# A three-layer block on one core: the recurrence's terms laid out apart, plain gathers with sums on VectorE, late weights issued by SyncE, and new durations for the order of instructions

## The chip, the cores and the metric

The kernel runs on one core of one Trainium2 chip. The metric is the device time of one execution in microseconds (us); lower is better. Everything is float32 except a few small masks. Five engines of the core each run their own list of instructions in order: PE (TensorE, matrix products and transposes), DVE (VectorE), ACT (ScalarE), POOL (GpSimd) and SP (SyncE, which here issues DMAs and reads registers). Each engine waits at an instruction until its inputs are there, and everything behind that instruction in its list waits too.

## The reference

An input x of 8 sequences by 512 positions by 128 channels passes through four residual layers: a gated-delta recurrence, a mixture of experts, a linear attention and the same mixture of experts again. Each layer sees a layer norm of x.

```python
# layer a: 16 heads of 8 channels; q, k, v pass a 4-tap causal convolution and silu; q and k are normalised
def step(S, inp):                                   # S: 8 x 8 per sequence and head
    q_t, k_t, v_t, b_t = inp
    v_new = (v_t - einsum('bhd,bhdm->bhm', k_t, S)) * b_t[..., None]
    S = S + einsum('bhd,bhm->bhdm', k_t, v_new)
    return S, einsum('bhd,bhdm->bhm', q_t, S)
...
# layers f and g: the two best of 8 experts for each row
topw, topi = top_k(softmax(xt @ Wg), 2)
topw = topw / sum(topw)
h = relu(einsum('nd,edf->enf', xt, W1)); y = einsum('enf,efd->end', h, W2)
out = einsum('ne,end->nd', combine, y)              # combine holds topw at topi
...
# layer b: linear attention of 16 heads with phi = elu + 1, causal
num = (tril(phi_q phi_k^T)) v + phi_q S;  den = the same with ones for v;  out = num / den
...
x = x + a(norm(x)); x = x + f(norm(x)); x = x + b(norm(x)); x = x + f(norm(x))
```

## The kernel before

**Tiling.** The 512 positions are cut into eight chunks of 64. A chunk of all eight sequences is 512 rows, held as a tile `x_a` of 128 partitions by 4 by 128. In the recurrence the 128 partitions are the 8 x 16 pairs of sequence and head instead, and the data of a chunk pass through DRAM (`scr`, `scb`, `sco`) to change between the two layouts.

**Streams.** The work is written as Python generators: `preparing` (norm, convolutions, the recurrence's factors, one chunk after another), `recurring` (the recurrence itself), and four `layers` lanes, each of which takes two chunks through the layers f, b and g. A generator yields the name of the engine that it needs next. `Weaver.run` (L97) takes, again and again, the stream that could start first by a clock that it keeps for each engine, using the durations of the function `duration` (L180) and ranks for ties. So the order of instructions on every engine is fixed when the program is built; on the chip each engine follows it. `Slots` hands out named buffers, and a stream that finds none free waits until one is given back.

**Preparing** (L491 to L682). `prepare(c)` loads `x_a`, takes the norm (`bn_stats` on DVE, four small `rs` operations on POOL, `xn` on ACT), transposes it, and multiplies it by four shifted weights `wc` for each of q, k and v (`s_pp_a`, tags s = 0, 1, 2), with `beta` beside it. Each result `y_a` goes out to `scr` and comes back as `qk` or `vv`. ACT then writes the squares `sq` and the turned copies `kq`. DVE forms the norms `nrm`, the factors `W`, and couples the four tokens of each step through the tiles `spare` and `kk`; two products of the second coupling run on POOL (L628). Products of queries and keys (`of_q`, L640) use the same tile tag `t8`. After chunk 0 `load_later_weights` (L326) issues, all on ACT's queue, the expert weights `w` to DRAM, the attention weights `wb`, `wob`, `bob`, and twelve blocks of zeros to the expert row buffers `there`. The six issues of `w` come from L329 and L331, the small weights from L334 to L336, the zeros from L355.

**Recurring** (L702 to L790). Four tokens make a step and four steps a group, so a chunk has four groups and the kernel 128 steps. The state is kept per group in one tile `st[p, step, term, m, d]` with five terms: four updates and the old state. Each step is four DVE instructions in a chain: product `pj`, its sum into `factors` (PSUM), the updates `st[:, s, 0:4]`, and a sum over the five terms into the next step's state:

```python
terms = st[:, s].rearrange("p i m d -> p m d i")
dve.tensor_reduce(st[:, s + 1, TK], terms, AX.X, ALU.add)
```

A term has 8 x 8 numbers, so the five numbers of one sum lie 256 bytes apart. `outputs` (L756) then copies the last state into its own group and the factors into `vn`, both on ACT; POOL multiplies states by queries into `po`, and DVE sums `po` into `o`. `ending` (L792) adds the corrections (`oc`), normalises (`so`, `rms`, `on`) and sends the result through `sco` to `oT`.

**Experts** (`moe`, L928). Each chunk's rows are sorted by expert: eight indirect DMAs on POOL scatter weighted rows `xw` to `there`; SP loads them back as `xs` in blocks; PE multiplies each block by its expert's weights `wt`, which SP fetches by register; the results go to `back`, and eight indirect DMAs gather them and add them to `x_a` in flight (L1189). Of the sixteen layers f and g, thirteen run so; g6, f7 and g7 run all experts densely (`all_experts`, L833) with weights that stay in SBUF. Each sorted layer owns one of three sets of buffers `m`.

**Attention** (`attend`, L1209). Per 128 rows POOL forms the products `kv`, PE multiplies them by a triangular matrix, DVE by the queries. `keep` (L1312) adds the chunk's keys and values to the running state `sbd`: DVE masks into `up`, POOL adds.

All four instructions of a step, all products and nearly every other instruction are issued through `Timed` and carry its line, L166; the profile's groups are told apart by tile names.

Of the kernel before, what the change touches and what calls it, by code (L numbers as in the profile page):

```python
# [179 lines left out]
def duration(key, op, args, kw):  # L180
# [6 lines left out]
    if key == "PE":  # L187
        if op == "transpose":
            return key, 0.16, 0.15
        return key, max(free_size(args[2]) * 1.95e-3, 0.32), 0.15  # L190
# [4 lines left out]
    if key == "ACT":  # L195
        table = TABLE_OF.get(args[2]) if op == "activation" else None
        return key, (0.39 if "bias" in kw else 0.2) + n * 0.76e-3, 0.1, table
    if key == "POOL":
        return key, 0.15 + n * (1.8e-3 if n > 512 else 2.2e-3), 0.1
    if op == "reciprocal":  # L200
        return key, 0.06 + n * 7.6e-3, 0.0
# [4 lines left out]
def kernel(  # L206
# [119 lines left out]
    def load_later_weights():  # L326
        for half in range(2):
            es = slice(half * NE // 2, (half + 1) * NE // 2)
            nc.scalar.dma_start(w12[es, :, 0:NF], f_w1[es])  # L329
            for f in range(2):  # L330
                nc.scalar.dma_start(  # L331
                    w12[es, :, NF + f * D : NF + (f + 1) * D], f_w2[es, f * P : (f + 1) * P, :]
                )
        nc.scalar.dma_start(wb, b_wT)  # L334
        nc.scalar.dma_start(wob, b_woT)
        nc.scalar.dma_start(bob, b_bo.to_broadcast([P, D]))  # L336
        nc.gpsimd.memset(earlier, 1.0)
# [12 lines left out]
        zero = slots.tile([P, 4 * D], F32, tag="m00", name="zero")  # L350
        nc.gpsimd.memset(zero, 0.0)
        for xd, _ in rows_by_expert:
            for g in range(0, NBK, 4):
                n = min(4, NBK - g)
                nc.scalar.dma_start(  # L355
                    blocks(xd)[:, g : g + n, :],
                    zero[:, 0 : n * D].rearrange("p (i d) -> p i d", i=n),
                )


    def held_in(n, shape, key, pool_=slots):
        return Slots(weaver, pool_, shape, key, n)

    banks = held_in(GENERAL, [P, 512], "s", ps)
    long_banks = held_in(7 - GENERAL, [P, 512], "y", ps)
    ys = held_in(2, [P, NB, CH], "y")
    sts = held_in(2, [P, SUB + 1, TK + 1, HD, HD], "st")
    pjs = held_in(2, [P, SUB, TK, HD, V1], "pj")
    pos = held_in(2, [P, 2, SUB, HD, HD], "po")
    mns = held_in(2, [P, 2 * D], "mn")  # L370
    phs = held_in(3, [P, 2 * D], "ph")
    vs = Slots(weaver, None, None, "v", 3, v1s)
    kvs = held_in(2, [P, NH, HD, HD], "kv")
    qss = held_in(1, [P, (NH + 2) * HD * HD], "qs")
    qTs = held_in(2, [P, P], "qT")
    nds = held_in(2, [P, ND + NH], "nd")
    dns = held_in(2, [P, NH], "dn")
    ups = held_in(2, [P, ND + NH], "up")
    xsTs = held_in(3, [P, HB * P], "xsT")
    hTs = held_in(3, [P, HB * P], "hT")  # L380
    ybs = held_in(2, [P, HB, D], "yb")
    xns = held_in(LANES + 1, [P, HB, D], "xn")
    ms = [held_in(3, [P, HB, D], f"m{i}") for i in range(SETS)]
    wts = held_in(SETS * WTS, [P, 2 * NF], "wt")
    ahead = [Slots(weaver, None, None, "ahead", AHEAD, list(range(AHEAD))) for _ in range(SETS)]
    sets = Slots(weaver, None, None, "set", SETS, list(range(SETS)))
# [104 lines left out]
    def prepare(c):  # L491
# [27 lines left out]
        sq = pair.tile([P, 2, CH, HD], F32, tag="t8", name=f"sq_{c}", bufs=1)  # L519
# [19 lines left out]
        def convolved(s):  # L539
            pp = yield from banks.take(f"pp_{n}_{s}")  # L540
# [16 lines left out]
            if s < 2:  # L557
                yield "ACT"
                act.activation(sq[:, s].rearrange("p t d -> p d t"), qk[:, s], AF.Square)
# [5 lines left out]
        landed = [spawn(beta())] + [spawn(convolved(s)) for s in (1, 0, 2)]  # L565
        qn, kn = kq[:, 0], kq[:, 1]
        for e in landed[1:3]:
            yield e
        yield "DVE"
        dve.tensor_reduce(nrm, sq, AX.X, ALU.add)  # L570
        yield "DVE"
        dve.tensor_scalar(nrm, nrm, ATT_A_EPS * ATT_A_EPS, None, ALU.max)
# [8 lines left out]
        nbr = pair.tile([P, CH], F32, tag="nbr", name=f"nbr_{c}", bufs=1)  # L581
        yield landed[0]
        yield "DVE"
        dve.scalar_tensor_tensor(br, be, 1.0, rk, ALU.add, ALU.mult)
        dve.scalar_tensor_tensor(nbr, br, -2.0, rk, ALU.mult, ALU.mult)
        yield "DVE"
        W = pair.tile([P, CH, 2 * HD], F32, tag="W", name=f"W_{c}")
        dve.tensor_tensor(W[:, :, 0:HD], kn, nbr.unsqueeze(2).to_broadcast([P, CH, HD]), ALU.mult)
        yield landed[3]
# [9 lines left out]
        spare = pair.tile([P, 2 * CH, HD], F32, tag="t8", name=f"spare_{c}", bufs=1)  # L599
        w01 = spare[:, 0:CH].rearrange("p t d -> p (t d)").rearrange("p (s d) -> p s d", s=NP)  # L600
        pr = spare[:, CH : CH + NP]
# [12 lines left out]
        pr = spare[:, 0:CH].rearrange("p (s i j) d -> p s i j d", i=2, j=2)  # L614
        for i in range(2):
# [8 lines left out]
        taken = [  # L624
            spare[:, i * CH : (i + 1) * CH].rearrange("p (s i w) d -> p s i (w d)", i=2, w=2)
            for i in range(2)
        ]
        for j in range(2):  # L628
            yield "POOL"
            pool.tensor_tensor(  # L630
                taken[j], W4[:, :, j, :].unsqueeze(2).to_broadcast([P, NS, 2, 2 * HD]),
                kk2[:, :, :, j].unsqueeze(3).to_broadcast([P, NS, 2, 2 * HD]), ALU.mult,
            )
        for j in range(2):
            yield "DVE"
            dve.tensor_tensor(W4[:, :, 2:4, :], W4[:, :, 2:4, :], taken[j], ALU.add)
# [3 lines left out]
        def of_q():  # L640
            pq = spare[:, 0:CH].rearrange("p (i s) d -> p i s d", i=TK)
# [10 lines left out]

    def preparing():
        yield spawn(weights_of_taps())
        for c in range(NCH):
# [6 lines left out]
            if c == 0:  # L662
                load_later_weights()
                spawn(centred(wg[:, 0:NE], NE, "wg"))
                spawn(centred(wb, 3 * D, "wb"))
# [7 lines left out]
        t = pair.tile([P, 2 * CH, HD], F32, tag="t8", name="w8", bufs=1)  # L673
        flat += [t[:, i * CH : (i + 1) * CH].rearrange("p t d -> p (t d)") for i in range(2)]
# [27 lines left out]
    def recurring():  # L702
        after = yield from sts.take("0_0")
        nc.vector.memset(after[:, 0, TK], 0.0)
        for c in range(NCH):
# [5 lines left out]
            vn = pair.tile([P, NS, TK, HD], F32, tag="vn", name=f"vn_{c}", bufs=1)  # L711
# [4 lines left out]
            for g in range(NS // SUB):  # L716

                s0 = g * SUB
                st = after
                last = c + 1 == NCH and g + 1 == NS // SUB  # L720
                if not last:
                    after = yield from sts.take(f"{c}_{g + 1}")
# [33 lines left out]
                def outputs(  # L756
                    st=st, c=c, g=g, s0=s0, op=op, qnp=qnp, vn=vn, vg=vg,
                    copied=None if last else after
                ):
                    if copied is not None:  # L760
                        yield "ACT"
                        act.copy(st[:, SUB, TK], copied[:, 0, TK])
                    yield "ACT"
                    act.copy(vn[:, s0 : s0 + SUB], vg)
# [19 lines left out]
                    yield from all_of([spawn(output(i)) for i in range(2)])  # L784
                    sts.give(st)
# [4 lines left out]
            spawn(ending(c, vn, o, op, nrm, qk, summed), -99)  # L790

    def ending(c, vn, o, op, nrm, qk, summed):  # L792
# [644 lines left out]
```

## Time and profile before

| | us |
|---|---|
| median of 3 runs (1055.51 to 1066.51) | 1059.97 |
| the profiled execution | 1058.37 |
| its span, first to last instruction | 1056.6 |

Mean granted TensorE clock in it: 0.82 of full speed. Busy time of the engines in stretches of the span, from the windows view (us):

| stretch | PE | DVE | ACT | POOL |
|---|---|---|---|---|
| 0 to 76 | 21.2 | 28.5 | 17.8 | 15.4 |
| 76 to 160 | 31.9 | 72.2 | 38.0 | 30.8 |
| 160 to 260 | 70.4 | 85.8 | 45.6 | 50.6 |
| 260 to 360 | 57.1 | 74.9 | 52.3 | 63.0 |
| 360 to 460 | 69.5 | 78.5 | 42.4 | 61.4 |
| 460 to 560 | 74.1 | 81.3 | 50.7 | 74.6 |
| 560 to 660 | 78.1 | 70.3 | 47.1 | 55.3 |
| 660 to 760 | 66.5 | 66.3 | 48.6 | 72.9 |
| 760 to 860 | 65.9 | 63.0 | 43.0 | 54.6 |
| 860 to 960 | 78.5 | 26.2 | 34.5 | 63.4 |
| 960 to 1057 | 76.9 | 24.5 | 31.6 | 23.1 |

How to read the lines: in a group of instructions, `out<-in` are the tiles by name, then the shapes and the count; after the first bar stand the busy time and the mean length of one in ns; after the second the idle time of the engine just before them, with what ended most of it. `SPq` and `ACTq` are DMA issues by those engines. A digit in the slices is the busy share in tenths of one of 40 equal slices of 26.4 us. The chain of waits is followed back from the last instruction, at each step to what released it, so its shares say what the end of the program hung on.

### The profile page before, as it was taken

Reading aid. Unit: us, or ns where it says so; the run is one execution under the profiler, and the core shown is the slowest. Engines: PE = TensorE matmul, PEld = TensorE weight load, DVE = VectorE, ACT = ScalarE, POOL = GpSimd, SP = SyncE. Lnnn points to the kernel's source line nnn. Section 1 sums busy time; section 2 is a strip of 40 time slices with the busy share of each in tenths; the row PEclk is TensorE's granted clock in tenths of the full one; section 3 lists DMA queues with packets and bytes.
Section 4 is the critical chain, followed back from the end, with each engine's and each line's share of the span. In section 5 each row is a group of like instructions: output and inputs, shape, how many; then the busy total and the mean of one; then the engine's idle time right before and its main releaser. Section 6 shows DMA issues by size and latency. Waiting matters only on the chain.

```text
span 1056.6 us, 12737 instructions
## 1 busy us (share of the span) xinstructions
PE 690.0 (65%) x3282; PEld 460.7 (44%) x3282; DVE 671.4 (64%) x1719; ACT 451.6 (43%) x1112; POOL 565.2 (53%) x626
## 2 busy tenths in 40 slices
PE   5114246667448597487678677748676807999867
PEld 2001116335446266277236565536345807444333
DVE  2538989789878489787879675648896411531610
ACT  3214264463526436366355454453533523434222
POOL 1212443654484835855892648785875275844230
PEclk9657577877768787798889988789688957999969
DMA  1252054343454542766443655764335555211010
GB/s 33 87 177 72 21 159 140 80 128 115 142 130 157 114 130 72 205 197 164 111 116 103 203 162 132 207 166 149 88 110 176 165 155 142 58 30 60 10 61 10
DMA packets 161097, 125.18 MB, mean 118 GB/s; under 512 B 45984, under 2 KB 126976, under 8 KB 161024
## 3 DMA queue, kind: packets, MB, share of 16 engines
q1 hardware_dynamic: 132640, 105.27, 33.8%
q0 software_dynamic: 18304, 13.64, 7.0%
q10 hardware_dynamic: 10080, 5.45, 1.7%
q8 instruction: 26, 0.43, 0.2%
q14 instruction: 47, 0.39, 0.1%
HBM read 90.98 MB, written 35.44 MB: 120 GB/s over the span
## 4 chain that ended last, share of the span: by engine, by line
DVE 32%; PE 22%; POOL 21%; issue 9%; ACT 6%; DMA 5%; ACTq 2%; another core or an unknown queue 1%; SPq 1%; POOLq 0%; DVEq 0%
POOL x_a L166 9%; DVE st L166 6%; PE y_py_g L166 4%; PE s_ph_g L166 4%; POOL po L166 4%; PE s_pp_a L166 3%; POOL there L166 3%; DVE factors L166 3%; PE s_pc_b L166 2%; DVE pj L166 2%; DVE nd_b L166 2%; DVE W L166 2%; DVE qs_b L166 2%; PE y_py_f L166 2%; DMA m_xs_g<-there 2%
## 5 line engine op out<-in xcount | busy, mean ns | idle before, releaser
L166 POOL TENSOR_TENSOR po<-st,kq 128x256 f32<-128x256 f32 x128 | 95.2, 871 | 68.0 <-DVE st L166 36.7
L166 PE MATMUL s_pc_b<-kv_b,tri 128*128 128x512 f32 x128 | 78.8, 730 | 38.9 <-POOL kv_b L166 38.6
L166 POOL DMA_INDIRECT x_a<-back,rows_f x56 | 88.3, 1576 | 17.9 <-issue 16.8
L166 PE MATMUL s_pp_a<-xnT_a,wc 128*128 128x512 f32 x192 | 97.6, 646 | 0.0
L166 DVE TENSOR_REDUCE st<-st 128x64 f32<-128x320 f32 x128 | 89.8, 701 | 3.8
L166 DVE TENSOR_REDUCE o<-po 128x64 f32<-128x512 f32 x64 | 43.5, 681 | 67.0 <-POOL po L166 67.0
L166 POOL DMA_INDIRECT x_a<-back,rows_g x48 | 75.1, 1564 | 17.6 <-issue 14.2
L166 PE MATMUL y_py_f<-wt_f,hT_f 128*128 128x128 f32 x420 | 65.3, 310 | 23.5 <-ACT hT_f L166 21.8
L166 POOL TENSOR_TENSOR kv_b<-ph_b,v 128x1024 f32<-128x1024 f32 x32 | 65.0, 2096 | 28.2 <-DVE ph_b L166 23.3
L166 POOL DMA_INDIRECT there<-m_xw_f,rows_f x56 | 56.2, 1004 | 31.8 <-issue 12.5
L166 PEld LDWEIGHTS y_py_f<-wt_f,hT_f 128*128 128x128 f32 x420 | 58.5, 218 | 27.8 <-ACT hT_f L166 24.4
L166 ACT ACTIVATE hT_g<-s_ph_g 128x512 f32<-128x512 f32 x80 | 46.3, 583 | 50.8 <-PE s_ph_g L166 49.0
L166 POOL TENSOR_TENSOR sbd<-sbd,up_b 128x144 f32<-128x144 f32 x48 | 27.5, 617 | 72.8 <-DVE up_b L166 72.6
L166 POOL DMA_INDIRECT there<-m_xw_g,rows_g x48 | 48.1, 1003 | 32.2 <-ACT m_xw_g L166 21.1
L166 DVE TENSOR_REDUCE factors<-pj 128x32 f32<-128x288 f32 x128 | 58.8, 459 | 9.7 <-ACT vn L166 5.6
L166 PE MATMUL s_ph_f<-xsT_f,wt_f 128*128 128x128 f32 x420 | 62.4, 303 | 1.8 <-ACT xsT_f L166 1.0
L166 DVE TENSOR_TENSOR qs_b<-s_pc_b,ph_b 128x512 f32<-128x512 f32 x64 | 43.1, 684 | 31.4 <-PE s_pc_b L166 31.4
L166 PE MATMUL s_pt_g<-ident,m_xs_g 128*128 128x128 f32 x106 | 21.8, 346 | 61.0 <-DMA m_xs_g<-there 59.5
L166 PE MATMUL y_py_g<-wt_g,hT_g 128*128 128x128 f32 x360 | 52.1, 297 | 14.2 <-ACT hT_g L166 14.1
L166 PEld LDWEIGHTS s_ph_f<-xsT_f,wt_f 128*128 128x128 f32 x420 | 57.4, 214 | 7.0 <-issue 2.9
L166 ACT ACTIVATE hT_f<-s_ph_f 128x512 f32<-128x512 f32 x72 | 40.5, 576 | 43.6 <-PE s_ph_f L166 35.5
L166 DVE TENSOR_TENSOR st<-factors,kq 128x256 f32<-128x256 f32 x128 | 54.0, 422 | 4.6 <-issue 1.3
(299 smaller groups left out, 1722.0 us busy)
## 6 DMA issues: line engine op xcount, KB each, us to landing
wt_f<-w SPq DMA_DIRECT2D x105, 256.0 KB
wt_g<-w SPq DMA_DIRECT2D x90, 256.0 KB
scr<-y_a SPq DMA_DIRECT2D x24, 256.0 KB
m_xs_f<-there SPq DMA_DIRECT2D x21, 256.0 KB
back<-yb_f SPq DMA_DIRECT2D x21, 256.0 KB
m_xs_g<-there SPq DMA_DIRECT2D x18, 256.0 KB
back<-yb_g SPq DMA_DIRECT2D x18, 256.0 KB
qk<-scr SPq DMA_DIRECT2D x16, 256.0 KB
```

What stands on the lines that cost most here:

```text
L166: r = call(*args, **kw)
```

## The change

1. `duration`: a transpose 0.2 us instead of 0.16, POOL's power 1.05, a reciprocal 0.15 + 6.5 ns per element, `bn_stats` 0.28.
2. The late weights become a stream on SP; small weights first, then `w`, then the zeros. The memsets that stood among them become part of this stream. The centring of `wb` waits for its load.
3. The state tile is `st[p, term, step x m x d + 16]`, read through `by_step`. The five numbers of one sum now lie 336 numbers, 1344 bytes, apart.
4. The convolutions run in the order keys, values, beta, queries, and wait for the taps' weights, which are formed beside the first norm. Norms of keys and queries are formed apart. The tag `t8` is split in two, `t80` and `t81`; four buffers `y` instead of two.
5. The coupling products `spare` run on DVE.
6. In the recurrence the copy of the last state goes from ACT to POOL, and `vn` is copied 2 us later by the weaver's clock. `vn` is taken once the chunk before has used its own; `oc` takes the tag `so`; `oT` has two buffers instead of three. `ending` waits for the chunk before to reach `delta`, and `sco` for `added` two chunks before.
7. The gathers go to buffers `g` without accumulation, and DVE adds each of the two to `x_a`.
8. The attention's running state is added on DVE, for both halves at once.

```diff
-    sts = held_in(2, [P, SUB + 1, TK + 1, HD, HD], "st")
+    sts = held_in(2, [P, TK + 1, (SUB + 1) * HD * HD + 16], "st")
+    def by_step(t):
+        t = t[:, :, 0 : (SUB + 1) * HD * HD]
+        return t.rearrange("p i (s m d) -> p s i m d", s=SUB + 1, m=HD)
...
+    def loading_later_weights():
+        for w, by in ((wb, b_wT), (wob, b_woT), (bob, b_bo.to_broadcast([P, D]))):
+            yield "SP"
+            sp.dma_start(w, by)
+        fire("wb")
...
+                yield "SP"
+                sp.dma_start(w12[es, :, to], by)
+                weaver.took("SP", 1.5)
...
+                yield "SP"
+                sp.dma_start(blocks(xd)[:, g : g + n, :], zero[:, 0:n, :])
...
-        landed = [spawn(beta())] + [spawn(convolved(s)) for s in (1, 0, 2)]
+        landed = [spawn(convolved(1)), spawn(convolved(2)), spawn(beta()), spawn(convolved(0))]
...
-            yield "POOL"
-            pool.tensor_tensor(
-                taken[j], W4[:, :, j, :].unsqueeze(2).to_broadcast([P, NS, 2, 2 * HD]),
+            yield "DVE"
+            dve.tensor_tensor(
+                taken, W4[:, :, j, :].unsqueeze(2).to_broadcast([P, NS, 2, 2 * HD]),
...
-                        yield "ACT"
-                        act.copy(st[:, SUB, TK], copied[:, 0, TK])
+                        yield "POOL"
+                        pool.tensor_copy(st[:, SUB, TK], copied[:, 0, TK])
...
+        if c > 0:
+            yield fired("delta", c - 1)
...
         for k in range(2):
+            g = yield from m_.take(f"g_{name}_{k}")
             for at in range(HB):
                 yield "POOL"
                 pool.indirect_dma_start(
-                    out=xt[:, at, :], out_offset=None, in_=yd,
+                    out=g[:, at, :], out_offset=None, in_=yd,
...
-                    compute_op=ALU.add,
...
+            def add(g=g, back=back):
+                weaver.goes_on(back)
+                yield "DVE"
+                dve.tensor_tensor(xt, xt, g, ALU.add)
+                m_.give(g)
...
-                        yield "POOL"
-                        pool.tensor_tensor(sb, sb, up, ALU.add)
-                        ups.give(up)
+                if c > 0:
+                    yield "DVE"
+                    dve.tensor_tensor(sb, sb, up, ALU.add)
+                    ups.give(up)
```

## The prediction

> **What bounds the kernel now.** The page's busy table and its forty slices come first, then the chain that ended last.
>
> ```profile
> PE 690.0 (65%) x3282; PEld 460.7 (44%) x3282; DVE 671.4 (64%) x1719; ACT 451.6 (43%) x1112; POOL 565.2 (53%) x626
> ...
> PE   5114246667448597487678677748676807999867
> DVE  2538989789878489787879675648896411531610
> ...
> POOL 1212443654484835855892648785875275844230
> ...
> DVE 32%; PE 22%; POOL 21%; issue 9%; ACT 6%; DMA 5%; ACTq 2%; another core or an unknown queue 1%; SPq 1%; POOLq 0%; DVEq 0%
> ```
>
> No engine is full over the whole span, and the slices show three stages. Up to slice 3 (76 us) little runs. From 76 to 560 us DVE is the fullest: the windows view gives it 72.2 of 84, 85.8, 74.9, 78.5 and 81.3 of each 100 us. From 560 to 860 us nothing is full (DVE 70, 66, 63; PE 78, 67, 66 per 100) and engines wait for each other in their fixed orders. After 860 us PE has 155 of 197 us. The chain passes between DVE, PE and POOL accordingly.
>
> Which groups the chain is made of:
>
> ```profile
> POOL x_a L166 9%; DVE st L166 6%; PE y_py_g L166 4%; PE s_ph_g L166 4%; POOL po L166 4%; PE s_pp_a L166 3%; POOL there L166 3%; DVE factors L166 3%; PE s_pc_b L166 2%; DVE pj L166 2%; DVE nd_b L166 2%; DVE W L166 2%; DVE qs_b L166 2%; PE y_py_f L166 2%; DMA m_xs_g<-there 2%
> ...
> L166 POOL DMA_INDIRECT x_a<-back,rows_f x56 | 88.3, 1576 | 17.9 <-issue 16.8
> ...
> L166 DVE TENSOR_REDUCE st<-st 128x64 f32<-128x320 f32 x128 | 89.8, 701 | 3.8
> L166 DVE TENSOR_REDUCE o<-po 128x64 f32<-128x512 f32 x64 | 43.5, 681 | 67.0 <-POOL po L166 67.0
> ...
> L166 POOL DMA_INDIRECT there<-m_xw_f,rows_f x56 | 56.2, 1004 | 31.8 <-issue 12.5
> ...
> L166 POOL TENSOR_TENSOR sbd<-sbd,up_b 128x144 f32<-128x144 f32 x48 | 27.5, 617 | 72.8 <-DVE up_b L166 72.6
> ```
>
> The accumulating gathers into x are the largest entry (9.1% in the chain view, 96 us); each holds POOL 1576 ns, a plain scatter 1004. A reduce of 320 elements takes 701 ns, more than one of 512 (681). POOL stands 72.6 us for `up` before `sbd`, with `po` products behind it, and DVE stands 67.0 us for `po`.
>
> Last, the timeline of the start:
>
> ```profile
> 46.32 0.65 ACTq L329 DMA_DIRECT2D w<-in_f_w_dram  x1
> ...
> 47.01 4.36 ACTq L331 DMA_DIRECT2D w<-in_f_w_dram  x2
> ...
> 51.40 3.19 ACTq L329 DMA_DIRECT2D w<-in_f_w_dram  x1
> ...
> 54.64 4.71 ACTq L331 DMA_DIRECT2D w<-in_f_w_dram  x2
> ...
> 59.39 2.93 ACTq L334 DMA_DIRECT2D wb<-in_b_wT_dram  x1
> ...
> 63.37 7.69 ACTq L355 DMA_DIRECT2D there<-zero  x12
> ...
> 73.31 0.69 DVE L166 TENSOR_REDUCE o<-po 128x64 f32<-128x512 f32 x1 [15.34 <-POOL po L166]
> ```
>
> ACT issues DMAs from 46.3 to 71.1 us. The copy of `st`, which POOL needs for `po`, is queued behind them, so DVE stands 15.3 us in the first recurrence. The four rs operations of chunk 1 are queued on POOL behind that `po` and start at 73.36, though their input is there at 57.4.
>
> **What the Trainium skill says.** (1) "SBUF — State Buffer", Door 1: SBUF has 16-byte lines, and an access that always goes to a new line pays. Within the trace this fits the 256-byte reads of the reduce, and also strided writes: `W<-vv` (64-byte steps) 1079 ns and `on` (256-byte) 1046, against 690 for a contiguous 512. By that sentence 1344 bytes is no better than 256. (2) "GPSIMD Engine Reference", 4.1 Engine selection: two-input elementwise work is about twice as slow on GpSimd as on VectorE. The trace says 1.6 times (`spare<-W,kk` 1142 on POOL, 697 on DVE). (3) The SBUF page, Who interferes with whom: a VectorE instruction with two SBUF inputs and a GpSimd one that reads SBUF block each other. `po` takes 714 ns at least and 871 in the mean, which agrees. (4) "DMA: Bandwidth & Descriptors", Issuing engines are not separate DMA queues: moving an issue to another engine saves sequencer time only. Here that time is ACT's 24 us.
>
> **The change part by part.** Sums are against the profiled execution, 1058.4 us (its span is 1056.6), 1.6 below the median of the runs, 1060.0.
>
> Start. The six `w`, three small weights and twelve zero blocks go from ACT to SP. The 15.3 us stall goes. Chunk 0's first steps also shorten: the third tap product (1.1) is no longer ahead of the statistics, beta's matmul (1.9) no longer ahead of the keys, keys and values no longer wait for the queries (`W` some 2 earlier), and `spare` stays on DVE (0.7): about 5.5. In the other direction, SP's order places a `w` (2.3, from 4.71/2) before chunk 1's keys and one of 3.2 before its values: +5. The zero blocks come after chunk 1's queries in SP's order, some 90 us in, and the first scatter at 143.9 needs them, so they are hidden; the memsets (2.5 us on POOL) lie beside the second recurrence group. Net -16, bounds -5 to -28 (chunk 1's transposes, at 75.9 now, could come as early as 60).
>
> Reduce of `st`. No read at 1344 bytes is in the trace. From 459 ns (288 elements) and 681 (512) contiguous reads cost 0.99 ns per element, so 320 would take 0.49 us: between 0 and 128 x 0.21 = 27 us of DVE. I take 0.49 despite point 1, because successive terms now fall 64 bytes apart modulo 256 instead of on the same offset; this is my weakest step. On the chain `st` has 6.2%, 65.5 us, of which reduces are 62% by busy time (89.8 of 143.8): 58 of them, -12.
>
> Gathers. Plain ones to `g`, 104 of them. Nearest row: the plain scatter, 1004 against 1576; between 1.0 and 1.55 us each, and 1.0 taken. 96 us on the chain is 61 gathers, x 0.57 = -35. Added: 26 DVE sums of 512 elements at 0.684, 17.8 us; each waits for landings, and what is queued behind it on DVE waits too. For some eight batches on the chain the last sum is 5.5 us, and of the other 12.3 DVE's third of the chain makes 4: +9. The accumulates of the second choice no longer need the first ones' landing; I give nothing for it. `g` takes `m` buffers that `xs` has left by then, so no new wait for a buffer.
>
> POOL to DVE. `spare` 16 x 0.69 and `sbd` 24 x 0.459 (by the 288-element row) add 22 us to DVE; a third to a half is on the path: +9. POOL loses 17.4 + 27.5 us and the two waits of 72.6 and 64.8 (28.6 of the latter at the start, where it held nothing up). Of DVE's 67.0 us for `po`, 51.6 lie after the start; I take half, -25 (bounds 0 and -50).
>
> ACT to POOL. The 31 copies of `st` leave ACT with 68.3 us of its waiting; POOL's waits for them, 31.0, include 16.7 already counted at the start. Half the rest, less 31 x 0.25 where POOL is on the path: -5. `vn` is written 2 us late by design; ending and `sco` get three more waits on the chunk before, which `on` at about 120, 291 and 476 us, some 170 us apart, should satisfy long before.
>
> Order. The new durations move instructions: the last chunk's recurrence starts after 80% of DVE's instructions instead of 75%, and g5 routes before `on` of chunk 7. Less then lies beside the tail, whose PE work (690 us in all) is unchanged. A gathering priced at 1.3 us costs 1.85 with its gap now and would cost 1.3, so the order would fit better. I enter 0, between -20 and +20. Halved norms, `br` in place, four `y` instead of two: under 2 us together, hidden by DMA landings.
>
> Sum: -16 - 12 - 35 + 9 + 9 - 25 - 5 = -75. One chain's savings aren't all kept: in 560 to 860 us the landings of `m_xs` and ACT's `m_xw` stand next, and after 884 us it is PE. I keep three quarters, about -57: **1001 for the profile, 1002 for the median**.
>
> **Rivals.** *VectorE becomes the bound (slower).* DVE gains 17.8 + 11.0 + 11.0 = 40 us where it is already 75 to 86% full. If the reduce stays at 0.70 and the gathers at 1.55, all 40 fall on the path against -16 at the start and some -12 of POOL waits: 1072. It decides once gathers stay above about 1.3 us and more than three quarters of the added DVE work is exposed. For it: the fullness. Against: 385 us of DVE idling, 67 of it on POOL's products. Chance 0.08. *The small gain.* The stride does nothing and the saved POOL time is mostly hidden, because DVE gives the pace: start -16, a third of the gathers -12, waits -10, added work +15: some 1037 (1025 to 1049). For it: point 1. Chance 0.23. *No change:* +40 meets the start and half the gathers, -35: 1060; 0.07. *The large gain.* All -75 is kept and the order fits, -20 more: 965 (945 to 980). Chance 0.22. Mine (980 to 1025) has 0.40.
>
> **How the numbers follow.** Below 945 and above 1046 I leave some 0.2 together: range 945 to 1046. About 1% is what a measurement here can tell from no change; faster is mine, the small and the large gain, 0.85; same 0.07; slower 0.08.
>
> **What would show it.** In the changed profile: ACT's stand of 24 us gone and chunk 1's transposes at or before 66 us; the `st` reduce near 0.49; the gathers near 1.0; DVE's wait for `po` halved; DVE at about 671 - 27 + 40 = 684 us busy. Gathers still at 1.5, or DVE above 90% with PE and POOL waiting for it, would make the forecast wrong.

## The result, and the profile after

| | median, us | runs | ratio to before |
|---|---|---|---|
| before | 1057.3 (1052.99 to 1066.51) | 20 | 1 |
| after | 1054.5 (1047.38 to 1058.45) | 20 | 0.996, 95% interval [0.9942, 0.9979] |

The changed kernel is some 4 us faster, where 58 were forecast. Its time lies above the forecast range of 945 to 1046 us.

First the page of the changed kernel: span, busy times, three rows of the forty slices, and the chain that ended last.

```profile
span 1051.4 us, 12743 instructions
...
PE 708.6 (67%) x3282; PEld 479.5 (46%) x3282; DVE 723.9 (69%) x1801; ACT 454.3 (43%) x1087; POOL 469.2 (45%) x593
...
PE   6150635757476883789577963779386868897967
...
DVE  2779878888789986778776898874778910373410
...
POOL 1141252661746607660574527750467413916130
...
DVE 38%; PE 30%; POOL 10%; issue 8%; DMA 6%; ACT 5%; SPq 2%; another core or an unknown queue 1%; ACTq 0%; POOLq 0%; DVEq 0%
```

POOL is 96.0 us less busy and its share of the chain has halved, from 21% to 10%. DVE is 52.5 us busier. What the chain no longer spends on POOL it spends on DVE and PE. DVE is also 40 us busier than the 684 us that were forecast. Slices 2 and 3 of DVE are fuller than before: the start has moved forward.

Now the groups that the change touches, from the view of groups with different shapes kept apart:

```profile
L166 DVE TENSOR_REDUCE st<-st 128x64 f32<-128x320 f32 x128 | 89.4, 699 | 3.7
...
L166 POOL DMA_INDIRECT m_g_f<-back,rows_f x56 | 55.0, 981 | 39.7 <-issue 16.1 <-DMA scr<-y_a 11.7 <-PE s_ph_g L166 9.3
...
L166 DVE TENSOR_REDUCE o<-po 128x64 f32<-128x512 f32 x64 | 43.3, 682 | 47.5 <-POOL po L166 47.4
...
L166 DVE TENSOR_TENSOR x_a<-x_a,m_g_g 128x512 f32<-128x512 f32 x12 | 17.9, 1490 | 4.5 <-DMA m_g_g<-back,rows_g 4.3 <-issue 0.2
L166 DVE TENSOR_TENSOR spare<-W,kk 128x512 f32<-128x512 f32 x24 | 17.7, 739 | 0.7
...
L166 DVE TENSOR_TENSOR sbd<-sbd,up_b 128x288 f32<-128x288 f32 x24 | 14.2, 592 | 0.8
L166 DVE TENSOR_TENSOR x_a<-x_a,m_g_f 128x512 f32<-128x512 f32 x14 | 14.1, 1005 | 25.1 <-DMA m_g_f<-back,rows_f 24.7 <-issue 0.4
```

The reduce of `st` takes 699 ns, against 701: the new distance of its five terms does nothing. A gather went from 1576 to 981 ns. DVE's wait for `po` fell from 67.0 to 47.4 us. By the timeline more than half of that fall lies at the start: up to the first result of chunk 0 it went from 18.5 to 7.0 us, where a single stall of 15.3 us is gone, and later from 48.5 to 40.5. The 26 sums of gathers cost 32.0 us of DVE, not 17.8, because a few are stretched; the view by tile gives least, median and longest:

```profile
L166 DVE TENSOR_TENSOR x_a<-x_a,m_g_f x14: 679/692/2646, 189.8 to 896.2; 128x512 f32<-128x512 f32 x14
L166 DVE TENSOR_TENSOR x_a<-x_a,m_g_g x12: 675/691/4948, 331.3 to 910.9; 128x512 f32<-128x512 f32 x12
```

The timeline shows what stands beside the longest one, two products on POOL:

```profile
331.27 4.95 DVE L166 TENSOR_TENSOR x_a<-x_a,m_g_g 128x512 f32<-128x512 f32 x1
331.81 3.85 POOL L166 TENSOR_TENSOR kv_b<-ph_b,v 128x1024 f32<-128x1024 f32 x2
```

It ends 0.56 us after them. By the timeline all seven sums that take over 0.7 us run beside POOL products of two inputs, and each ends some 0.56 us after one of these has ended.

The timeline shows when each chunk has its first result added to `x_a` (start of the instruction, us), and the last product `pj` of the recurrence:

| chunk | before | after | after, old table (e3) | best version (e16) |
|---|---|---|---|---|
| 0 | 130.0 | 116.1 | 117.0 | 123.6 |
| 1 | 196.8 | 187.8 | 189.2 | 189.8 |
| 2 | 299.5 | 294.5 | 289.3 | 290.7 |
| 3 | 368.1 | 365.5 | 385.8 | 352.7 |
| 4 | 491.6 | 475.0 | 491.4 | 468.7 |
| 5 | 583.6 | 622.0 | 601.7 | 559.1 |
| 6 | 721.8 | 737.0 | 695.6 | 690.9 |
| 7 | 840.9 | 857.6 | 812.6 | 803.4 |
| last `pj` | 810.8 | 831.2 | 790.5 | 772.9 |
| end of the span | 1056.6 | 1051.4 | 1019.3 | 1003.8 |

After chunk 0 the changed kernel is 14 us ahead, after chunk 4 still 17; by chunk 5 it is 38 us behind. The last two columns belong to experiments. The gain of the start is real. Where it is lost, these marks can't show, because the two kernels order their work differently. The recurrence is late from chunk 5 on, but work of the later layers is early: the third result of layer b is added to `x_a` at 495.2 us instead of 565.7, the fifth at 723.4 instead of 772.3. At 800 us PE has begun 2508 of its 3282 matmuls, and 2411 before; at 900 us it is 2888 and 2864. After the last `pj` 220 us follow, against 246 before.

### The profile page after: what moved, and what is told of

It is laid out like the page before. It is cut to its first block, busy times and chain, and to the rows that moved or that the text cites. A ratio compares the mean times of both kernels' runs of the same rounds, so it can differ in the third digit from the quotient of the medians.

```text
span 1051.4 us, 12743 instructions
## 1 busy us (share of the span) xinstructions
PE 708.6 (67%) x3282; PEld 479.5 (46%) x3282; DVE 723.9 (69%) x1801; ACT 454.3 (43%) x1087; POOL 469.2 (45%) x593
## 4 chain that ended last, share of the span: by engine, by line
DVE 38%; PE 30%; POOL 10%; issue 8%; DMA 6%; ACT 5%; SPq 2%; another core or an unknown queue 1%; ACTq 0%; POOLq 0%; DVEq 0%
DVE st L166 6%; PE s_pc_b L166 5%; PE s_ph_g L166 5%; PE y_py_g L166 4%; POOL po L166 4%; PE s_pp_a L166 3%; DVE W L166 3%; DVE factors L166 3%; DVE pj L166 3%; DVE spare L166 2%; PE y_py_f L166 2%; SPq L166 2%; DVE nd_b L166 2%; PE s_ph_f L166 2%; DVE qs_b L166 2%
## 5 line engine op out<-in xcount | busy, mean ns | idle before, releaser
L166 PE MATMUL s_pp_a<-xnT_a,wc 128*128 128x512 f32 x192 | 101.7, 667 | 2.7 <-ACT xnT_a L166 2.7
L166 POOL TENSOR_TENSOR po<-st,kq 128x256 f32<-128x256 f32 x128 | 90.3, 735 | 0.6
L166 DVE TENSOR_REDUCE o<-po 128x64 f32<-128x512 f32 x64 | 43.3, 682 | 47.5 <-POOL po L166 47.4
L166 POOL DMA_INDIRECT m_g_f<-back,rows_f x56 | 55.0, 981 | 39.7 <-issue 16.1
L166 PE MATMUL s_ph_f<-xsT_f,wt_f 128*128 128x128 f32 x420 | 68.2, 322 | 6.4 <-issue 3.8
L166 PE MATMUL y_py_g<-wt_g,hT_g 128*128 128x128 f32 x360 | 55.6, 309 | 19.8 <-ACT hT_g L166 12.4
L166 PEld LDWEIGHTS s_ph_f<-xsT_f,wt_f 128*128 128x128 f32 x420 | 62.7, 232 | 10.5 <-issue 4.9
L166 PEld LDWEIGHTS y_py_g<-wt_g,hT_g 128*128 128x128 f32 x360 | 50.0, 215 | 28.8 <-ACT hT_g L166 18.2
L166 ACT ACTIVATE hT_f<-s_ph_f 128x512 f32<-128x512 f32 x72 | 40.6, 574 | 48.5 <-PE s_ph_f L166 41.8
L166 PEld LDWEIGHTS s_pp_a<-xnT_a,wc 128*128 128x128 f32 x192 | 38.1, 213 | 45.9 <-issue 39.2
```

The source lines that it names most:

```text
L166: r = call(*args, **kw)
```

## The experiments

The theory at this point (A): the parts that shorten POOL's work and the start gain what the forecast said, the stride nothing, and the loss comes from the order that the weaver makes anew. Its rival (B): the work that DVE takes over lies on the path and eats the gain. A second rival (C): POOL's time was hidden, so that plain gathers gain little. The chips used differ by about 1% in the time of the same kernel; every ratio below is to the kernel before on the same chip. "Order kept" means that the weaver's clock is told the old duration and engine, so that the other engines' lists stay as they were.

**m1: the reduce by itself.** The program copies `x` to the output and computes nothing else of the reference; DVE runs reduces of 64 sums over data of different spacing.

```diff
+    for lo in (64, 320, 336, 324, 65):
+        v = src[:, 0 : 5 * lo].rearrange("p (i s) -> p i s", i=5)[:, :, 0:64].rearrange("p i s -> p s i")
+        nc.vector.tensor_reduce(r, v, AX.X, ALU.add)
...
+    for n in (2, 3, 4, 5, 8, 16):
+        v = src[:, 0 : 64 * n].rearrange("p (s i) -> p s i", i=n)
...
+    for n in (2, 8):
+        v = src[:, 0 : 64 * n].rearrange("p (i s) -> p s i", i=n)
```

> This leaves out the whole computation: x is copied to the output, and VectorE runs reduces on constant data, eight of each: five numbers per sum at 256, 260, 1280, 1296 and 1344 bytes apart, contiguous sums of 2, 3, 4, 5, 8 and 16 numbers, and sums of 2 and 8 numbers 256 bytes apart, 64 sums each. Theory A (every step to a new 16-byte line pays, whatever the stride): contiguous five 0.49 us, all strided fives 0.70. Theory B (a sum has a least price of some 8 elements, the stride costs nothing): contiguous five 0.70 us too, contiguous 8 0.68, contiguous 2 also near 0.65. Theory C (the prediction's: only strides of a multiple of 256 bytes pay): 0.70 at 256 and 1280, 0.49 at 1344, 1296 and 260.

The view by tile gives least, median and longest of all forty sums over five at the five distances (256, 1280, 1344, 1296 and 260 bytes); the groups below it compare neighbours with numbers 256 bytes apart:

```profile
L59 DVE TENSOR_REDUCE five<-src x40: 679/681/710, 5.2 to 30.1; 128x64 f32<-128x320 f32 x40
```

```profile
L69 DVE TENSOR_REDUCE apart<-src 128x64 f32<-128x512 f32 x8 | 8.1, 1010 | 0.2
L64 DVE TENSOR_REDUCE contiguous<-src 128x64 f32<-128x512 f32 x8 | 5.4, 675 | 0.0
L64 DVE TENSOR_REDUCE contiguous<-src 128x64 f32<-128x320 f32 x8 | 3.8, 475 | 0.0
...
L69 DVE TENSOR_REDUCE apart<-src 128x64 f32<-128x128 f32 x8 | 2.2, 276 | 0.0
L64 DVE TENSOR_REDUCE contiguous<-src 128x64 f32<-128x128 f32 x8 | 2.2, 274 | 0.0
```

No distance differs from another by more than 31 ns. Only terms that are neighbours get the 0.48 us on which the forecast counted. Pairs pay nothing for the distance.

**e1: plain gathers alone.** The kernel before without accumulation, in its own order; the gathered rows replace `x` instead of being added.

```diff
-                    compute_op=ALU.add,
```

> The kernel before with its gathers no longer accumulating, and nothing else: same order of instructions on all engines, no sums on VectorE. It leaves out the sums into x (x is overwritten by the second choice's row). POOL is relieved of 104 x 0.57 = 60 us. If that relief lay on the path (the prediction's step), 35 us faster than before: some 1022. If VectorE sets the pace and POOL's time was hidden by it, less than 15 us faster: 1042 or more.

998.89 us against 1047.51, ratio 0.9538 [0.9518, 0.9558]: 48.6 us for one line. From its page:

```profile
PE 683.2 (68%) x3282; PEld 457.0 (46%) x3282; DVE 671.4 (67%) x1719; ACT 451.7 (45%) x1112; POOL 502.8 (50%) x626
...
DVE 38%; PE 27%; POOL 11%; issue 8%; DMA 6%; ACT 6%; ACTq 2%; SPq 2%; POOLq 0%; DVEq 0%
...
L166 POOL DMA_INDIRECT x_a<-back,rows_f x56 | 55.0, 982 | 16.7 <-issue 14.3
```

POOL is busy 62.4 us less, and the program is 48.6 us shorter: C falls. Earlier arrival of the gathered rows may have a part in it: before, PE and its weight loads stood 6.7 and 8.7 us for these rows at the transposes of layer b, and in e1 they don't. The run doesn't separate the two, but these waits, 15.4 us together, are too short to make up the 48.6. The chain looks like that of the changed kernel (DVE 38%, POOL 11%), yet the program is 50 us shorter. The same chain shares go with quite different times.

**e2 and e2b: less work of DVE in the recurrence.** The sum over five terms takes two of them, in the changed kernel (e2) and in the kernel before (e2b), order kept; three terms are left out of the state.

```diff
-                    terms = st[:, s].rearrange("p i m d -> p m d i")
+                    terms = st[:, s, 3:5].rearrange("p i m d -> p m d i")
```

> The changed kernel with the recurrence's sum over two of its five terms, the weaver still counting five, so that the order of instructions is the same. It leaves out three of the five terms. VectorE is relieved of some 128 x 0.3 to 0.4 = 40 to 50 us. If VectorE sets the pace, 25 to 45 us faster than the changed kernel: 1010 to 1030. If the new order is what holds it (waits between engines, not VectorE's work), less than 15 us: 1040 or more.

> The kernel before with the recurrence's sum over two of its five terms and the weaver counting five: the same order. It leaves out three of the five terms. VectorE loses some 53 us, as in the same cut of the changed kernel (which gave 3.6% there). If VectorE's work was paid at the same 0.7 in the kernel before, 35 us faster; if the accumulating gathers on POOL set the pace there, 15 us or less.

e2: 0.9599 [0.9572, 0.9626], 3.6% less than the changed kernel, some 38 us for the 53.5 us that DVE lost: 0.7 us per us. e2b: 0.9861 [0.9829, 0.9893], 15 us for 52: 0.3. In the changed kernel DVE's chain of steps counts for more than twice as much. The two kernels differ in every part and in their order, so which of these does it isn't shown. It speaks for B as far as the recurrence goes; what follows asks it of the work that the change added.

**e10: the sums nearly free.** The 26 sums add one channel of 128, order kept.

```diff
-                dve.tensor_tensor(xt, xt, g, ALU.add)
+                nc.vector.tensor_tensor(xt[:, :, 0:1], xt[:, :, 0:1], g[:, :, 0:1], ALU.add)
+                weaver.took("DVE", 0.16 + 512 * 1.04e-3, 0.0)
```

> The changed kernel with each sum of gathered rows over one of 128 channels instead of all, the weaver still counting the whole, so that the order is the same and all readers still wait for the gathers. It leaves out 127 of 128 channels of what the experts add. VectorE loses some 32 - 26 x 0.17 = 27 us. If VectorE's added work is paid at 0.7, 19 us faster than the changed kernel; if the sums lie beside other work, less than 8.

0.9948 [0.9935, 0.9961], 0.1% below the changed kernel and not to be told from it, although the sums take 10.3 us instead of 32.0 and DVE as a whole is 14 us less busy (710.1). The length of the sums is not what eats the gain: B falls for them. Two of them are stretched still, to 4.3 and 2.1 us, so their waits for POOL are only partly gone.

**e5, e12 and e12p: gathers and sums, with a new and with the old order.** e5 puts part 7 of the change into the kernel before and lets the weaver order everything anew. e12 makes the same instructions, but the sums go to DVE without the weaver's clock knowing of them: PE, ACT and SP have exactly the lists of before, DVE these 26 sums more. e12p is e12 with the sums on POOL.

```diff
             def add(g=g, back=back):
                 weaver.goes_on(back)
-                yield "DVE"
-                dve.tensor_tensor(xt, xt, g, ALU.add)
+                yield None
+                nc.vector.tensor_tensor(xt, xt, g, ALU.add)
                 m_.give(g)
```

> The kernel before with part 7 of the change alone: plain gathers into buffers and their sums on VectorE (the weaver makes a new order with them). By the run that only made the gathers plain (4.6% faster than before in the old order) and a price of some 0.7 us of time per us added to VectorE (26 sums, 18 to 32 us): 25 to 36 us faster than before, plus or minus 20 for the new order. If the sums eat the whole gain, within 10 us of before.

> The kernel before with plain gathers and their sums on VectorE, as in the run with part 7 alone, but with every other instruction in the order of before: the weaver doesn't count the sums, and PE, ACT and SP have exactly their old lists. If the sums or their waits for landings ate the gain of the gathers, within 10 us of before. If the newly made order ate it, most of the 4.6% of the plain gathers stays: 20 to 45 us faster than before.

> The same with the 26 sums on POOL, some 1.27 us each, at the same places. POOL is relieved of 60 - 33 = 27 us only, and waits for landings with other work behind it: if POOL's relief is what counts, some half of the gain of the version with sums on VectorE, 10 to 20 us faster than before.

e5: 0.9997 [0.9978, 1.0016]. e12: 0.9663 [0.9624, 0.9702]. e12p: 0.9761 [0.9732, 0.9789]. e5 and e12 do the same work; between them lies only the place of instructions, and it costs 3.3%, some 35 us. This is A, shown on one part of the change. It also prices the sums with their waits: from e1 to e12 1.25%, 13 us, where +9 was forecast.

**e3 and e14: the duration table.** e3 is the changed kernel with the old table, e14 the kernel before with the new one and nothing else.

```diff
-            return key, 0.16, 0.15
+            return key, 0.2, 0.15
+    if key == "POOL" and ALU.pow in args:
+        return key, 1.05, 0.1
-        return key, 0.06 + n * 7.6e-3, 0.0
+        return key, 0.15 + n * 6.5e-3, 0.0
+    if op == "bn_stats":
+        return key, 0.28, 0.0
```

> The changed kernel with the four entries of the duration table set back: only the order of instructions differs. If the new durations gave back what the rest of the change had gained, 20 us or more faster than the changed kernel: under 1035. If VectorE's load is the cause, within 10 us of it, 1045 to 1065.

> The kernel before with the new duration table: only the order of instructions differs. If the new durations make a worse order in general, 10 us or more slower than before. If the loss of 2% that they made in the changed kernel is a matter of how each order happens to fall, it may go either way here: between -20 and +20, as likely faster as slower.

e3: 0.9768 [0.973, 0.9806], 2% or 20 us below the changed kernel. e14: 1.0452 [1.0422, 1.0481], 47 us slower, with the same instructions but for three more loads of function tables on ACT. DVE's take as long as before (672.4 us busy, 671.4 before), PE's longer (709.3, 690.0 before). Its longest waits of the whole span, from the view of waits (us in total, times, longest):

```profile
ACT qT_b L166 <- PE s_pt_q_b L166: 116.5, 21, 18.1
PEld s_pc_b L166 <- POOL kv_b L166: 115.1, 16, 19.1
PE s_pc_b L166 <- POOL kv_b L166: 109.2, 12, 17.9
```

Before, these three were 50.5, 44.1 and 38.6 us. Attention's matmuls stand in PE's list and wait for the POOL products that they need.

**f1, f2, f3, f5 and f9: which entry.** The new table gives a power on POOL 1.05 us, and the kernel still books 0.8 us after each power by hand (L457 and L484 of the changed kernel), so the clock counts 1.85 where 1.04 to 1.08 is measured, and counted 0.96 before. The theory (P) was that this double entry spoils the order; the rival (R), that any change of an entry reshuffles some hundreds of places and the time scatters. f1 is the changed kernel and f2 is e14, each without the 0.8; f3 is the kernel before with the power's entry alone, f5 with the transposes' entry alone; f9 is the changed kernel with the transposes' entry set back.

```diff
         pool.tensor_tensor(rs[:, 0], rs[:, 0], mhalf, ALU.pow)
-        weaver.took("POOL", 0.8)
```

```diff
-            return key, 0.16, 0.15
+            return key, 0.2, 0.15
```

> The changed kernel without the two entries of 0.8 us that the planner books on POOL after each power; the new table already gives a power 1.05 us, so it is now booked once (1.05 where 1.04 to 1.08 is measured) and not 1.85. Theory P (the power booked twice is what spoils the new order): the time falls to that of the changed kernel with the old table, ratio to before about 0.977. Theory R (the newly made order scatters by several per cent with any change of the table, without regard to how true an entry is): anywhere between 0.96 and 1.03, and no nearer to 0.977 than to 0.996.

> The kernel before with the new table, and the two entries of 0.8 us after the powers gone. With them the new table costs 4.5% (1.0452). Theory P: most of this goes, ratio 0.99 to 1.01. Theory R: anywhere between 0.97 and 1.05.

> The kernel before with one entry of the new table alone: a power on POOL is 1.05 us, with the 0.8 us after it left (1.85 in all, 0.96 before). Theory P: most of the 4.5% of the whole new table, ratio 1.03 to 1.05. Theory R: anywhere between 0.97 and 1.05.

> The kernel before with another entry of the new table alone: a transpose is 0.2 us instead of 0.16. It makes about as many instructions change their place as the power's entry does. Theory P: within 1% of before, 0.99 to 1.01. Theory R: it can move the time by as much as the power's entry, 2 to 5% either way.

> The changed kernel with one entry of the table set back: a transpose is booked at 0.16 us again, not 0.2; power, reciprocal and bn_stats stay new. Theory T (the transpose entry is what spoils the order, since alone it costs the kernel before 2.1%): the ratio to before falls to about 0.977, as with the whole old table. Theory R (any change of the table reshuffles some hundreds of places in each engine's list, and the time scatters by some per cent): anything from 0.97 to 1.03, and not tied to the sign seen in the kernel before.

| table | work of before | work of after |
|---|---|---|
| old | 1 | 0.9768 (e3) |
| new | 1.0452 (e14) | 0.996 |
| new, power booked once | 1.0543 [1.0518, 1.0569] (f2) | 1.0053 [1.0034, 1.0072] (f1) |
| old, power's entry new | 0.9979 [0.9959, 0.9999] (f3) | not tried |
| old, transposes' entry new | 1.0209 [1.0177, 1.0241] (f5) | not tried |
| new, transposes' entry old | not tried | 0.995 [0.9934, 0.9965] (f9) |

P falls: booking the power once makes both kernels 0.9% slower, and the double entry alone costs nothing. The transposes' entry alone costs the kernel before 2.1%, but setting it back leaves the changed kernel where it was. No entry that was tried carries the loss; those of the reciprocal and of `bn_stats` were not tried alone. In a column the program does the same work and only the order differs, and the times spread over 5.6% and 2.8%. In both columns the old table, less true to the chip, makes the best order or one within 0.2% of it (f3). Why it does is open. The order also decides how often ACT loads a function table, 1.28 us each time: 35 times before and in e3, 41 in the changed kernel, 42 in e5, 47 in f5. That alone doesn't explain the times: f1 has 36 loads and is the slowest of its column.

The waits of f9, whose time is that of the changed kernel within 0.1%, show how little a single wait tells here:

```profile
ACT qT_b L166 <- PE s_pt_q_b L166: 90.5, 19, 12.0
PEld s_pc_b L166 <- POOL kv_b L166: 85.2, 12, 22.2
PE s_pc_b L166 <- POOL kv_b L166: 79.1, 12, 21.6
```

And the same three in the changed kernel:

```profile
ACT qT_b L166 <- PE s_pt_q_b L166: 51.7, 18, 9.9
...
PEld s_pc_b L166 <- POOL kv_b L166: 32.8, 13, 8.7
...
PE s_pc_b L166 <- POOL kv_b L166: 23.6, 7, 8.1
```

PE's wait for `kv_b` is three times as long in f9, at the same time in total. So the waits of e14 above are what its order looks like, and not shown to be the cause of its 47 us.

**e11 and f4: the products against the plan.** In the changed kernel the weaver plans the `spare` products and the `sbd` sums for DVE, and e11 issues them on POOL. f4 is e16 (next), in which the weaver plans them for POOL, and issues them on DVE. The other engines keep their lists.

```diff
-            dve.tensor_tensor(
+            nc.gpsimd.tensor_tensor(
+            weaver.took("DVE", 0.16 + 512 * 1.04e-3, 0.0)
```

```diff
-                        pool.tensor_tensor(sb, sb, up, ALU.add)
+                        nc.vector.tensor_tensor(sb, sb, up, ALU.add)
+                        weaver.took(*duration("POOL", "tensor_tensor", (sb, sb, up, ALU.add), {}))
```

> The changed kernel with the 16 coupling products and the 24 sums of the running state on POOL again, all other instructions in the same order and the weaver still counting VectorE. VectorE loses 11 + 14 = 25 us, POOL gains some 17 + 22 us and waits for VectorE within them. If VectorE's added work is paid at 0.7, up to 18 us faster; if POOL's waits for VectorE held up the products behind them, as the prediction had it, that takes back 10 or more, and the time stays within 8 us of the changed kernel or gets longer.

> The kernel before with its own order kept: plain gathers with sums on VectorE and late weights issued by SyncE (0.956 so far), and now also the taken products and the sums into sbd on VectorE, in the places the planner gives them as if they were on GpSimd. If what the product parts gain in the changed kernel (about 9 us) holds in the old order too, 0.945 to 0.950; if their 22 us on VectorE fall on its full stretch, 0.957 to 0.965.

e11: 1.0045 [1.0025, 1.0065], 9 us slower than the changed kernel. f4: 0.9686 [0.9643, 0.9728], 13 us slower than e16, although each instruction is much faster on DVE, as the groups of f4 show (on POOL in e16 `sbd` takes 516 ns and `spare` 1071):

```profile
L1341 DVE TENSOR_TENSOR sbd<-sbd,up_b 128x144 f32<-128x144 f32 x48 | 17.9, 376 | 0.6
...
L630 DVE TENSOR_TENSOR spare<-W,kk 128x512 f32<-128x512 f32 x16 | 10.8, 685 | 0.2
```

The same instructions lose in either direction when they leave the engine that they were planned for. What parts 5 and 8 are worth by themselves can't be read from either run.

**e16: the late weights, and the best version.** e12 with the late weights issued by SP instead of ACT, at the same place of the program and all else as it was.

```diff
-            nc.scalar.dma_start(w12[es, :, 0:NF], f_w1[es])
+            nc.sync.dma_start(w12[es, :, 0:NF], f_w1[es])
```

> The version with plain gathers and sums on VectorE in the order of before, and the late weights issued by SP at the same place of the program; nothing else is moved. The start should give its 15 us on top: 15 (10 to 20) us faster than the version without. If later waits absorb the earlier start, less than 5.

1003.83 us, 0.956 [0.9519, 0.9601]: another 1.0% or some 10 us below e12, and 4.4% below before. From its page:

```profile
span 1003.8 us, 12782 instructions
...
PE 678.5 (68%) x3282; PEld 453.8 (45%) x3282; DVE 693.8 (69%) x1745; ACT 450.9 (45%) x1112; POOL 507.0 (51%) x626
```

It takes part 7 and the main point of part 2 (the issuing engine, not the new order of the loads), leaves the order alone, and beats both kernels and e3. By the table of chunks it is ahead of the kernel before at every mark.

## Why the prediction was wrong

**The start: right.** -16 forecast. Chunk 0 is added 13.8 us earlier in the changed kernel, chunk 1's transposes begin at 56.8 us instead of 75.9, and moving the late weights alone is worth some 10 us in time (e12 to e16). What of it the changed kernel keeps to its end isn't measured.

**The reduce: wrong.** "I take 0.49 despite point 1": it is 0.699, and by m1 no distance would have helped. The term was -12 and is 0, and the 27 us of DVE time that it was to save are the larger part of the 40 us by which DVE is busier than forecast; the rest is near the 14 us of the stretched sums. The Trainium skill's sentence in "SBUF — State Buffer", Door 1, that an access which always goes to a new line pays, was the better guide than an argument from offsets modulo 256. In m1 it held for sums over five and over eight, but not for pairs (0.276 us apart, 0.274 as neighbours).

**The gathers: right in mechanism, too small.** 1.0 us for a plain one was right (0.98). -35 was worked out from the chain's share; e1 measured -48.6 in the old order. The chain had named 61 of the 104 gathers; all of them became 0.59 us shorter, 61 us together, and the program became shorter by some four fifths of that, part of it perhaps through earlier arrivals (see e1).

**The sums: +9, measured 13** (e1 to e12).

**POOL to DVE: the waits did not come back as time.** Of DVE's wait for `po` outside the start 51.6 us were known, and half of it, -25, was taken. After chunk 0 this wait fell by 8.0 us only. Point 2 of the prediction, about twice as slow on GpSimd, holds for `sbd`: 2 x 617 ns there for what DVE does in 592; for `spare` it is 1142 and 739, 1.5 times. But the time is +13 us in one order and -9 in the other, by which engine the plan had in mind. The copy of `st`, for which -5 was entered, now holds POOL up for 96.0 us in 14 waits for DVE; what that costs was not tried alone.

**The order: the step that failed.** "so the order would fit better. I enter 0, between -20 and +20." A table nearer to the chip did not make a better order: with it the changed kernel is 20 us slower than with the old one (e3), at the outer bound of the term, and the kernel before 47 us slower (e14), far beyond it. The entry of 0 was argued from the price of one instruction, the gather's 1.3 us, while every change of the table moves hundreds. And it priced the new table alone: every other part of the change makes the weaver order anew as well, which cost 35 us in e5 and had no term in the sum.

**The balance.** Forecast -58, measured -4 (0.4% of 1057). What is missing, 54 us: 20 are the new table (e3). 9 to 12 are the reduce, at the size that the forecast gave it (12, or 9 of the three quarters that it kept). The other 22 to 25 are not measured separately, and parts 4 and 6 were not tried alone. e5 shows that a newly made order can cost 35 us even with the old table, so that this is their likely place, with DVE's waits for POOL that stayed; it is not shown. In the old order two parts alone give -46 (e16), while the whole change with the old table and a new order gives -25 (e3), so the forecast misjudged not so much what the work is worth as what the ordering takes.

**The rivals.** "No change" came near the measured time by a wrong mechanism, and so by luck: it had the added work of DVE meet half the gathers. Its own terms, +40 and -35, make some 1065 and not 1060. The gain of the gathers is whole in e1, and the length of the sums is nothing in e10. "VectorE becomes the bound" is half true: its share of the chain rose from 32 to 38%, and a microsecond of its recurrence is now worth 0.7 instead of 0.3 (e2, e2b).

**One reading of the profile was wrong as well.** The mean of 871 ns of `po`, against 714 at least, was put down to DVE and POOL blocking each other, as the Trainium skill's "SBUF — State Buffer", Who interferes with whom, says of instructions with two SBUF inputs beside GpSimd's reads. In e1 DVE has the same list and `po` takes 737 ns, `sbd` 507 instead of 617, so most of the stretching went with the accumulating gathers. Of the 32 `po` that take over 0.9 us before, 30 stand in eight groups right behind such a gather, as here:

```profile
197.97 1.54 POOL L166 DMA_INDIRECT x_a<-back,rows_f  x1 [0.30 <-issue]
198.97 3.35 POOL L166 TENSOR_TENSOR po<-st,kq 128x256 f32<-128x256 f32 x4
```

The group begins before the gather has ended, and within it the products start 0.68 to 0.69 us apart, as if each were short: their records overlap. Blocking as in point 3 does fit the stretched sums of the changed kernel, which end when a product on POOL has ended.

## What to carry to other kernels

Where a planner fixes the order of instructions, measure a change with the old order held fixed first, and only then let the planner order anew: its order alone was worth up to 5.6% here, more than any single edit that was tried, and truer durations did not make it better. Take an accumulation out of gathers when the engine that issues them is on the path, and let another engine add. Before a layout is changed for a stride, time the one instruction by itself.

## What the hardware showed

- An indirect DMA that accumulates held POOL for 1.56 to 1.58 us, a plain one 0.98, with the same indices and sizes (before and e1).
- A reduce over five numbers at any of five distances from 256 to 1344 bytes took 0.68 us for 64 sums, and 0.475 over neighbours; over eight it is 1.010 against 0.675, over two 0.276 against 0.274.
- Seven of 26 sums of gathered rows on DVE took 0.98 to 4.95 us instead of 0.69. Each ran beside a POOL product of two inputs and ended some 0.56 us after it (the changed kernel). e10 shows that the length of the sums costs the program nothing here.
- 3282 matmuls took 719.7, 708.6, 690.0 and 678.5 us in f2, the changed kernel, the kernel before and e16, at a granted TensorE clock of 0.780, 0.807, 0.820 and 0.844 of full speed. The clock goes with the time of the whole program only roughly: e3, at 1019.3 us, has 0.815, below the 0.820 of the kernel before at 1056.6. Which of the two follows the other is open.
